# 3x3 convolution by tiles of 4x4 outputs for four images at once, in place of 4x2 outputs for two

**Chip, cores, metric.** One core of a Trainium2 chip. The time is that of one execution on the device in microseconds (us); the kernel before was run three times for its time and once with the profiler, every other kernel four times, one of them with the profiler, beside the kernel before on the same chip. The rounds ran on several chips, on which the median of the kernel before lay between 2524.8 and 2529.0 us: runs of different rounds are compared by their ratio to it, and a few us between their medians are not read as a difference.

## The reference, cut

Two bottleneck blocks, fp32, on 16 images of 1024 channels and 32x32 pixels. The first has local attention over 3x3 neighbours in its middle (32 heads of 8 channels), the second a 3x3 convolution of 256 channels.

```python
# layer 0
h = relu(bn(conv1x1(x, w_conv1)))                      # 1024 -> 256
q, k, v = relu(bn(conv1x1(h, wq))), relu(bn(conv1x1(h, wk))), bn(conv1x1(h, wv))
attn = softmax(einsum('bgdhw,bgdkhw->bgkhw', q, unfold3x3(k) + pos), axis=2)
a = relu(bn(einsum('bgdkhw,bgkhw->bgdhw', unfold3x3(v), attn)))
r = relu(bn(conv1x1(a, w_conv3)) + x)                  # 256 -> 1024
# layer 1
h1 = relu(bn(conv1x1(r, w1)))                          # 1024 -> 256
y = relu(bn(conv3x3(h1, w2)))                          # 256 -> 256, padding 1
out = relu(bn(conv1x1(y, w3)) + r)                     # 256 -> 1024
```

## The kernel before: the parts concerned

The program is one list of stages in TensorE's order. P is one image's projections (first 1x1, then q and k, then v; written C, Q, V when split), F a fused stage (256 to 1024, residual, and 1024 to 256 of layer 1), W a 3x3 stage, U the outputs of one image. While TensorE runs them, VectorE does the attention of other images "beside" them; a small model in the generator (`Side`) reckons with constants where VectorE will be, and so decides where each of its jobs goes in the programs' orders. Every engine and every transfer queue works in its own order: in the trace of the changed kernel TensorE's 6152 passes, VectorE's 1633 operations and ScalarE's 871 activations start in the order of their programs, by source line, and so do the 275, 490 and 512 transfers that ScalarE, SyncE and GpSimd issue.

The 3x3 convolution is done on transformed data (Winograd's method): weights (U) and input (V, the "form") are transformed, TensorE multiplies them, and VectorE transforms the products back to y. Other names in the profile lines: x is the input, h the output of a first 1x1, kp, bnk and bnv are keys and values on their way through DRAM (the "relay", which rearranges them), a is the attention's result, s a tile that holds the residual and then a fused stage's output, r the stored residual or the output, z a copy of products out of PSUM, diag a diagonal matrix for scaling the output weights. A "seed" is ScalarE's copy of the residual into PSUM, to which TensorE then adds. A "joint" is a place where one stage passes into the next.

```python
NI, NU = 6, 4                       # 6x4 products for a tile of 4x2 outputs
TR, TC = H // 4, W // 2
hpool: bufs=3 (8 KB)   ppool: bufs=4 (8 KB)   zpool: bufs=1, sized by tag

"P0 P1 P2 P3 F0 P4 C5 F1 Q5 W0 V5 U0 U1 F2 P6 C7 F3 Q7 W2 V7 U2 U3",
"F4 P8 F5 C9 Q9 W4 V9 U4 U5",
# ... [cut]
"F14 F15 U13:45 W14 U13:67 U14 U15",

# the form of the input is made piece by piece beside the products of its own stage
def along(t):
    v = ppool.tile([P, NU, NW * 2, TILES], F32, tag="t", name="v")
    # ... [cut: four VectorE operations with steps of two over the pixels]

# products: one product's 2 x 2 blocks of channels; 2 images x 128 tiles = 256 columns a pass
nc.tensor.matmul(acc[i][:, at, n, :], pieces[key][:, m, column % 2, n * P : (n + 1) * P],
                 vs[i][:, j, 2 * m : 2 * m + 2, :].rearrange("p b t -> p (b t)"), ...)

# end of a 3x3 stage, in the program's order
following[0][0].seed(following[0][1])      # ScalarE: residual into PSUM for the next output
finish_winograd(b)                         # ScalarE: batch norm and relu over y, two passes
if then:
    following[1][0].seed(following[1][1])
    finish_winograd(b + 1)

# logits of the attention end with
nc.vector.tensor_tensor(e, e, mx..., ALU.subtract)
yield None
nc.scalar.activation(e, e, AF.Exp)         # ScalarE, in its own order
```

Of the kernel before, what the change touches and what calls it, by code (L numbers as in the profile page):

```python
# [35 lines left out]
NI, NU = 6, 4  # L36
TR, TC = H // 4, W // 2
TILES = TR * TC
# [24 lines left out]
def sa_bottleneck_kernel(ctx: ExitStack, tc: tile.TileContext, x, w1t, wqkvt, w3t, u1t, u2t, u3t, params, out):  # L63
# [7 lines left out]
    hpool = ctx.enter_context(tc.tile_pool(name="hpool", bufs=3))  # L71
    apool = ctx.enter_context(tc.tile_pool(name="apool", bufs=1))
    ppool = ctx.enter_context(tc.tile_pool(name="ppool", bufs=4))
    zpool = ctx.enter_context(tc.tile_pool(name="zpool", bufs=1))
# [8 lines left out]
    uw = dram.tile([NI, 2, P, NW, 2, WID], F32, tag="uw", name="uw")  # L83
    ws = dram.tile([2, 2, P, NW, C // 2], F32, tag="ws", name="ws")

    COLUMNS = (1, 2, 3, 0)
# [15 lines left out]
    def more_weights():  # L102
# [4 lines left out]
        t = wpool.tile([P, HW], F32, tag="w", name=f"{name}{half}_{of}")  # L107
# [7 lines left out]
        if of == 0 and name == "w1":  # L115
            for c in range(k):
                nc.sync.dma_start(view[:, c], src[:, c])
        else:
            nc.sync.dma_start(view, src)
# [79 lines left out]

    VROWS = H + 4  # L200
    vh = const.tile([P, NW * 2 * VROWS + 2, PW], F32, tag="vh", name="vh")

    scaled = {}

    def load_scaled():

        rooms = vh.rearrange("p r w -> p (r w)")
        for which, src in enumerate((w3t, u3t)):
            for half in range(2):
                at = rooms[:, (2 * which + half) * HW :][:, :HW].rearrange("p (n o) -> p n o", n=NW)  # L210
# [6 lines left out]
    def scale_weights(which):  # L217
# [3 lines left out]
        diag = ppool.tile([P, 2 * HW], F32, tag="t", name="diag")[:, :C]  # L221
# [17 lines left out]

    taps = []  # L240

    def load_taps():
        n = 3 * WID
        for m in range(NW):
            pool, tag = ((ppool, "t"), (hpool, "h"))[m]
            first, second = (pool.tile([P, 2 * HW], F32, tag=tag, name="g") for _ in range(2))
            g = first[:, :n], first[:, n : 2 * n], second[:, :n]
            for i in range(3):
                nc.scalar.dma_start(g[i], u2t[m * P : (m + 1) * P, i * n : (i + 1) * n])
            taps.append(g)  # L250

    made = []

    def store_winograd_weights(of):
        for _ in range(of):
            m, i, half, u = made.pop(0)
            nc.sync.dma_start(uw[i, half][:, m], u)

    def winograd_weights():
        n = 3 * WID  # L260

        rooms = []
        for pool, tag, shape, of in (
            (apool, "e", [P, KK, JPIX], 1), (apool, "pc", [P, NPOS, JPIX], 1),
            (apool, "bnv", [P, HEAD_DIM, HALO], 1), (zpool, "tv", [P, NW * 2 * (TR + 1), PW], 2),
            (zpool, "m1", [P, NW, 2 * TILES], 4), (zpool, "s", [P, NW, 2 * TILES], 2), (wpool, "w", [P, HW], 2),
        ):
            for _ in range(of):
                t = pool.tile(shape, F32, tag=tag, name="u", **({"bufs": of} if pool is zpool else {}))
                if len(shape) == 3:  # L270
                    t = t.rearrange("p a b -> p (a b)")
                elif len(shape) == 4:
                    t = t.rearrange("p a b c -> p (a b c)")
                size = t.shape[1]
                rooms += [t[:, at : at + 2 * WID] for at in range(0, size - 2 * WID + 1, 2 * WID)]
        third, fourth = (ppool.tile([P, 2 * HW], F32, tag="t", name="g") for _ in range(2))
        s, t = third[:, :n], third[:, n : 2 * n]
        two = fourth[:, :n], fourth[:, n : 2 * n]
        small = third[:, 2 * n : 2 * n + WID], third[:, 2 * n + WID : 2 * n + 2 * WID]

        def both(dst, s, t, by):

            for to, op in zip(dst, (ALU.add, ALU.subtract)):
                nc.vector.scalar_tensor_tensor(to, s, by, t, ALU.mult, op)
# [844 lines left out]
```

## Time and profile before

| kernel before | |
|---|---|
| time | 2526.98 us, median of 3 runs (2520.68 to 2528.53) |
| span of the profiled run | 2520.6 us |
| TensorE / VectorE / ScalarE busy | 2470.8 / 1955.5 / 924.5 us |
| TensorE idle | 49.8 us |
| granted TensorE clock, mean | 0.998 |
| DMA | 638.9 MB, 253 GB/s |

The lines themselves, and how they are read, are in the prediction.

### The profile page before, as it was taken

To read this page: it belongs to the slowest core of one execution; us is meant where nothing else is said; L and a number is where in the kernel's file an instruction comes from. 1 tells how busy PE (TensorE), PEld (TensorE's weight loads), DVE (VectorE), ACT (ScalarE), POOL (GpSimd) and SP (SyncE) were. 2 spreads that over 40 slices of the span, in tenths; PEclk is the share of its full clock that TensorE was granted. 3 is DMA by queue.
4 is the path that set the end of the run, shared out by engine and by line. 5 is a ranking of instruction groups with operands and counts; after the bars stand their busy time and mean duration, and the time that the engine had idled before them with its cause. 6 is when DMAs were issued, how large, how long until landed. Compare 5 with 4: busy or idle time off the path is not lost.

```text
span 2520.6 us, 18901 instructions
## 1 busy us (share of the span) xinstructions
PE 2470.8 (98%) x6536; PEld 1224.1 (49%) x6536; DVE 1955.5 (78%) x1791; ACT 924.5 (37%) x891; POOL 239.5 (10%) x451
## 2 busy tenths in 40 slices
PE   7999999999999999999999999999999999899999
PEld 3443444644455444554445544455445544464464
DVE  6897999899989898989979991899814980993070
ACT  1224133552335524254232542325432533345335
POOL 1020110011000110001110011100100010001000
PEclk9999999999999999999999999999999999999999
DMA  8977677696776977678686777767767768658546
GB/s 304 352 252 258 232 266 238 208 371 235 265 246 228 344 243 259 219 256 327 230 276 228 274 258 252 253 220 273 278 211 236 255 233 269 218 200 303 189 150 234
DMA packets 244719, 638.87 MB, mean 253 GB/s; under 512 B 18576, under 2 KB 125328, under 8 KB 236432
## 3 DMA queue, kind: packets, MB, share of 16 engines
q0 software_dynamic: 63360, 266.89, 30.7%
q1 hardware_dynamic: 141152, 227.83, 28.4%
q10 hardware_dynamic: 40112, 142.94, 14.0%
q8 instruction: 53, 0.87, 0.1%
q14 instruction: 42, 0.34, 0.0%
HBM read 408.47 MB, written 229.11 MB: 253 GB/s over the span
## 4 chain that ended last, share of the span: by engine, by line
PE 84%; DVE 10%; DMA 3%; ACT 2%; issue 1%; ACTq 0%; SPq 0%; DVEq 0%; POOLq 0%
PE ps L387 31%; PE ps L356 30%; PE ps L738 12%; PE ps L437 10%; DVE prod L545 2%; DMA bnk<-kp 2%; DVE acc L609 1%; DVE term L597 1%; PE ps L480 1%; DVE v L665 1%; DVE prod L549 1%; DMA bnk<-bnk 1%; ACT h L956 1%; DVE tv L659 1%; DVE prod L550 1%
## 5 line engine op out<-in xcount | busy, mean ns | idle before, releaser
L356 PE MATMUL ps<-s,u 128*128 128x512 f32 x1024 | 458.4, 592 | 4.3 <-ACT s L400 4.3
L387 PE MATMUL ps<-a,w 128*128 128x512 f32 x1024 | 457.7, 592 | 0.0
L356 PE MATMUL ps<-x,w 128*128 128x512 f32 x1024 | 444.5, 595 | 9.5 <-DMA x<-in_x_dram 9.5
L387 PE MATMUL ps<-y,u 128*128 128x512 f32 x1024 | 441.6, 592 | 3.1 <-ACT ps L380 3.1
L545 DVE TENSOR_TENSOR prod<-qc,bnk 128x2048 f32<-128x2048 f32 x144 | 328.9, 2284 | 137.3 <-DMA bnk<-bnk 136.7
L738 PE MATMUL ps<-v,U 128*128 128x256 f32 x1536 | 338.1, 382 | 18.3 <-issue 7.3
L738 PEld LDWEIGHTS ps<-v,U 128*128 128x128 f32 x1536 | 292.4, 191 | 66.6 <-issue 13.1
L356 PEld LDWEIGHTS ps<-x,w 128*128 128x128 f32 x1024 | 195.4, 191 | 255.3 <-issue 244.9
L356 PEld LDWEIGHTS ps<-s,u 128*128 128x128 f32 x1024 | 194.3, 190 | 250.3 <-issue 235.1
L387 PEld LDWEIGHTS ps<-y,u 128*128 128x128 f32 x1024 | 194.4, 190 | 247.8 <-issue 222.4
L387 PEld LDWEIGHTS ps<-a,w 128*128 128x128 f32 x1024 | 194.6, 190 | 244.9 <-issue 226.0
L400 ACT ACTIVATE s<-ps,par 128x1024 f32<-128x1024 f32 x128 | 142.4, 1112 | 449.8 <-PE ps L387 449.8
L609 DVE TENSOR_TENSOR acc<-acc,term 128x2048 f32<-128x2048 f32 x128 | 293.3, 2292 | 4.4
L597 DVE TENSOR_TENSOR term<-e,bnv 128x2048 f32<-128x2048 f32 x128 | 292.2, 2283 | 0.0
L437 PE MATMUL ps<-h,wqk 128*128 128x512 f32 x512 | 230.4, 598 | 6.1 <-ACT h L956 6.1
L549 DVE TENSOR_TENSOR prod<-prod 128x1024 f32<-128x1024 f32 x144 | 176.3, 1224 | 4.9
L659 DVE SCALAR_TENSOR_TENSOR tv<-vh 128x1224 f32<-128x1224 f32 x32 | 45.0, 1426 | 167.8 <-ACT vh L990 167.8
L400 ACT ACTIVATE r<-ps,bn_sh 128x1024 f32<-128x1024 f32 x128 | 141.9, 1109 | 80.1 <-PE ps L387 79.4
L956 ACT ACTIVATE h<-ps,par 128x1024 f32<-128x1024 f32 x32 | 38.5, 1204 | 338.6 <-PE ps L356 338.6
L437 PEld LDWEIGHTS ps<-h,wqk 128*128 128x128 f32 x512 | 94.7, 190 | 138.9 <-issue 114.4
L380 ACT ACTIVATE ps<-s 128x1024 f32<-128x1024 f32 x128 | 131.4, 1027 | 56.4 <-ACT s L400 39.8
L335 POOL DMA_DIRECT2D r<-r x128 | 67.5, 528 | 888.5 <-DMA out_dram<-r 364.4
(93 smaller groups left out, 1725.5 us busy)
## 6 DMA issues: line engine op xcount, KB each, us to landing
s<-in_x_dram POOLq DMA_DIRECT2D x128, 512.0 KB, 5.8
r<-s ACTq DMA_DIRECT2D x128, 512.0 KB, 3.8
r<-r POOLq DMA_DIRECT2D x128, 512.0 KB, 5.0
out_dram<-r ACTq DMA_DIRECT2D x128, 512.0 KB, 6.1
x<-in_x_dram POOLq DMA_DIRECT2D x120, 512.0 KB, 4.3
U<-uw SPq DMA_DIRECT2D x96, 512.0 KB, 3.8
bnk<-kp SPq DMA_DIRECT2D x32, 680.0 KB, 7.2
bnv<-kp SPq DMA_DIRECT2D x32, 680.0 KB, 6.8
```

Of the source, the lines that this page charges most:

```text
L335: (nc.scalar if kind == "x" and b == 0 else nc.gpsimd).dma_start(t, src)
L356: nc.tensor.matmul(ps[n][:, halves(half)], wt[:, c % (NC // 2), n * P : (n + 1) * P], src[:, halves(half)], start=(c == 0), stop=(c == NC ...
L380: nc.scalar.activation(ps, t, AF.Identity)
L387: nc.tensor.matmul(self.ahead[o][:, halves(half)], pieces[key][:, n, o % (NC // 2) * P :][:, :P], self.src[:, n, halves(half)], start=Fals ...
L400: nc.scalar.activation(t, self.ahead.pop(o), RELU, bias=self.shift(o), scale=1.0)
L437: nc.tensor.matmul(ps[:, halves(half)], pieces[key][:, m, at : at + P], h[:, m, halves(half)], start=(m == 0), stop=(m == NW - 1),)
L545: nc.vector.tensor_tensor(by_row(t), by_row(qc), kc[:, :, i : i + JROWS, j : j + W], ALU.mult)
L549: nc.vector.tensor_add(t[:, 0:4], t[:, 0:4], t[:, 4:8])
L597: nc.vector.tensor_tensor(by_row(dst), rows(e[:, k, :]).unsqueeze(1).to_broadcast([P, HEAD_DIM, JROWS, W]), vc[:, :, i : i + JROWS, j : j ...
L609: nc.vector.tensor_add(acc, acc, t)
L659: nc.vector.scalar_tensor_tensor(to, a, by, b, ALU.mult, ALU.add)
L738: nc.tensor.matmul(acc[i][:, at, n, :], pieces[key][:, m, column % 2, n * P : (n + 1) * P], vs[i][:, j, 2 * m : 2 * m + 2, :].rearrange("p ...
```

## The change

The intent is a shorter TensorE stream: tiles of 4x4 outputs need a quarter fewer products, and with four images at once a pass keeps its 256 columns (the count is in the prediction). To make the form of the input contiguous for VectorE, layer 1's pixels are kept by their column's place in a tile (columns 0, 4, 8... first); ScalarE makes this order on the way out of PSUM. The form is now made right behind each fused stage, stored to DRAM and loaded when the 3x3 stage comes; images 13 and 14 are put off through a stash in DRAM. The buffers are cut anew, the forming of the 3x3 weights is interleaved with the first projections, and the exponential is issued by the model of VectorE.

```diff
-NI, NU = 6, 4
-TR, TC = H // 4, W // 2
-TILES = TR * TC
+NI = 6
+NK = 4
+TR = H // 4
+TILES = TR * TR
-    hpool = ctx.enter_context(tc.tile_pool(name="hpool", bufs=3))
+    hpool = ctx.enter_context(tc.tile_pool(name="hpool", bufs=5))
-    ppool = ctx.enter_context(tc.tile_pool(name="ppool", bufs=4))
-    zpool = ctx.enter_context(tc.tile_pool(name="zpool", bufs=1))
+    ppool = ctx.enter_context(tc.tile_pool(name="ppool", bufs=2))
+    zpool = ctx.enter_context(tc.tile_pool(name="zpool", bufs=3))
... [cut: weights' forming with ScalarE steps, weight pieces shared between stages]
         def result(self, o, to):
             t = self.tiles.pop(o)
-            nc.scalar.activation(t, self.ahead.pop(o), RELU, bias=self.shift(o), scale=1.0)
+            ps, to_ = self.ahead.pop(o), t
+            if self.kind == "s":
+                ps, to_ = ps.rearrange("p (n j) -> p j n", j=4), t.rearrange("p (j n) -> p j n", j=4)
+            else:
+                ps, to_ = ps.rearrange("p (j n) -> p n j", j=4), t.rearrange("p (n j) -> p n j", j=4)
+            nc.scalar.activation(to_, ps, RELU, bias=self.shift(o), scale=1.0)
... [cut: attention's adds by two taps]
-        yield None
-        nc.scalar.activation(e, e, AF.Exp)
-        yield 3.0
+        yield lambda: nc.scalar.activation(e, e, AF.Exp)
... [cut: the form, 24 operations of 612 or 816 elements, and its store]
+                nc.sync.dma_start(
+                    room[:, at // 2, :, b % NK, at % 2].rearrange("i p e -> p i e"),
+                    u.rearrange("p (i e) -> p i e", i=NI),
+                )
... [cut: products of four images, the way back on VectorE]
+    DEFERRED = 13, 14
... [cut]
+        "P0 P1 P2 P3 F0 P4 F1 P5 P6 F2 P7 F3 C8 Q8 W0 V8 U0 U1 U2 U3",
+        "F4 P9 F5 P10 F6 F7 C11 Q11 W4 V11 U4 U5 U6 U7",
+        "F8 P12 F9 P13 F10 F11 C14 Q14 W8 V14 U8 U9 U10:0123",
+        "F12 P15 F13 F14 F15 U10:4567 U11:012345 W12 U11:67 U12 U13 U14 U15",
... [cut]
+            if made:
+                finish_winograd(made.pop(0))
             cost = next(parts)
... [cut]
             following[0][0].seed(following[0][1])
             finish_winograd(b)
+            made.extend(range(b + 1, b + NK))
             if then:
                 following[1][0].seed(following[1][1])
-                finish_winograd(b + 1)
+                finish_winograd(made.pop(0))
```

## The prediction

> **What bounds the kernel now.** I read the page's busy shares and slices first, then its chain, the groups by line, the chain in order of time around one 3x3 stage, and last the stretches of 3x3 and output stages.
>
> ```profile
> PE 2470.8 (98%) x6536; PEld 1224.1 (49%) x6536; DVE 1955.5 (78%) x1791; ACT 924.5 (37%) x891; POOL 239.5 (10%) x451
> PE 84%; DVE 10%; DMA 3%; ACT 2%; issue 1%; ACTq 0%; SPq 0%; DVEq 0%; POOLq 0%
> ```
>
> TensorE is busy 2470.8 of 2520.6 us and is 84% of the chain: only what shortens its stream, or the 49.8 us in which it idles, is worth time. VectorE's 78% is a mean over stages, and matters where TensorE waits for it.
>
> ```profile
> L738 PE MATMUL ps<-v,U 128*128 128x256 f32 x1536 | 338.1, 382 | 18.3 <-issue 7.3
> L665 DVE TENSOR_TENSOR v<-tv 128x512 f32<-128x512 f32 x192 | 120.1, 687 | 2.3
> L659 DVE SCALAR_TENSOR_TENSOR tv<-vh 128x1224 f32<-128x1224 f32 x32 | 45.0, 1426 | 167.8 <-ACT vh L990 167.8
> L400 ACT ACTIVATE r<-ps,bn_sh 128x1024 f32<-128x1024 f32 x128 | 141.9, 1109 | 80.1 <-PE ps L387 79.4
> ```
>
> L738 is the 3x3 convolution of layer 1; the 382 ns of one is latency of a pipelined instruction, its pace must come from the chain:
>
> ```profile
> 432.02 41.44 PE ps L738 x192
> 473.46 6.87 PE ps L437 x16
> ...
> 2194.74 1.12 ACT r L400
> 2195.86 0.82 issue
> 2196.69 3.75 PE ps L738 x8
> ```
>
> 192 passes in 41.44 us are 0.2158 us a pass of 256 columns; 16 passes of 512 in 6.87 us are 0.429. The last lines are one of the few places where TensorE waited: a 3x3 stage that began late. Each 3x3 stage is followed by outputs:
>
> ```profile
> 432.00:473.50 41.50, 41.50 (x194) 36.53 (x193) 37.27 (x61) 10.52 (x17) 0.00 (x0) 1.00 0.58 170
> 480.30:542.10 61.80, 61.80 (x146) 27.36 (x145) 56.08 (x33) 42.54 (x40) 9.99 (x19) 1.00 0.99 362
> ```
>
> The columns are PE, PEld, DVE, ACT, POOL busy, clock, DMA share, GB/s. Both stretches keep TensorE full. The 3x3 stage has DMA to spare (0.58); the output stage has none (0.99).
>
> [...]2048 elements 2284 to 2292[...], 512 elements 687 to 692[...], for adds with two inputs and scaled sums alike. [...]Steps of two fp32 cost nothing here (L665 steps by two, 687 ns, the contiguous L550 692); a step of four, which the change brings to ScalarE's PSUM reads, no row shows. [...]the highest 20 us stretch here has 421 GB/s at a share of 1.02.
>
> **The change, part by part.** Tiles of 4x4 outputs in place of 4x2 need 36 products per 16 outputs where 24 per 8 stood. Four images (4x64 tiles) keep 256 columns a pass. Built, the program has 576 matmuls there in place of 768, two passes each.
>
> TensorE. Before 1536 x 0.2158 = 331.5 us (8 stages of 41.44), after 1152 x 0.2158 = 248.6 (4 of 62.2): **82.9 us less**. All other matmuls are the same in number and size. Their stages from the chain: one image's projections 50.83 us (71.62 to 122.45), fused stage 128 x 0.4293 = 54.95, outputs 64 x 0.4293 = 27.47. 16 x 133.25 + 331.5 = 2463.5, so 57.1 of the span lies outside the streams: about 20 at both ends and in the start (9.5 first input, 2.6 slow clock, 3.3 for the scale row, some 5 after the last matmul), the rest around the 3x3 stages and in small waits. After: 2132.0 + 248.6 = **2380.6, plus 20**.
>
> VectorE. Attention's adds go by two taps: 144 x (1224+692+425) = 337 us becomes 64 x 4208 + 16 x 2341 = 307: -30. The form was 256 us (rows of v and tv); it becomes 12 ops of 612 and 12 of 816 per image, 21.6 us, 346 in all: +90. The way back was 157 us (rows of y, m, s); per group of four it becomes 6 x 1.224 + 18 x 0.692 + 12 x 0.685 + 32 x 0.692 + 2 x 2.29 = 54.7 us, 219 in all: +62. Sum 1955.5 + 122 = some 2077, 84% of the new span. It remains second. Adding stages up, attention finishes well before its fused stage except for image 15: two fused stages and the value projection (117 us) stand between its queries and its use, against 13 for the relay, 94.2 of attention and some 15 back: about 5 us of wait.
>
> The 3x3 stage itself. A part is 16 passes, 3.45 us. VectorE's 54.7 us fit into 62.2 only if evenly spread, and they are not: it can start at 11.5 us (second copy out), and the middle pair brings 22 us (two sums of 2048, sixteen updates, the tile sums) after its last product at 41.4, so it ends at 58. The third pair's second tile sum then frees the copy buffer (three, each shared) late: the last part waits until 61.6, not 58.7: **2.9 us**. The y are complete from 71 us on, TensorE ends at 65.1, the value projection covers up to 72. Then ScalarE has, in program order, two finishing passes (1.23 each) for each of four images, two kp and two seeds between them, so the third output waits for its seed until about 85 where it could have begun at 79: **6.5 us**. In all 9.4 per stage, some 12 for the last one, which has two output parts as cover: **41 us in four**. Before, such ends were hidden because two images finish in half the ScalarE time.
>
> The entry of a 3x3 stage. Form and DRAM round trip replace the form beside the products. After the fourth image: 2.4 (vh) + 21.6 + about 8 (three v buffers, so two pairs wait for their store to land) + 5 store + 5 load = 42 us; the projections between are 43.6. It fits. For the last group only 10 output parts (34.3 us) lie between: **8 us**.
>
> DMA. The form stores 40.1 MB and loads 40.1; U loads fall by 12.6 MB, output weights by 4.2, stashes of two images add 5.3, the rest +1.3: 638.9 becomes some 709 MB, 288 GB/s. In the 3x3 stage U and V need 36 tiles of 0.53 MB, 14 of them fetched ahead: with the next stage's prefetch about 256 GB/s, against 170 before. Outputs of four images then run 110 us on end at the share of 0.99 that they had for 62.
>
> Sum: 2380.6 + 20 + 41 + 8 + 5 + 8 (kp, halo and other small waits; the old ones around 220 and 2190 us were of that size) = 2462.6 for the span; runs lie some us above it or at it. **I predict 2462 us**, 2.6% less: the gain of 83 is partly given back, about 20 us, at the joints.
>
> **Rivals.** (1) *The whole gain arrives.* If the author's order hides the ends (VectorE's rows overlap by some per cent: the rows add up to 1999, busy is 1955), the four stages lose 3 us each, not 10: 2425 to 2435. For it: before, TensorE waited only 18.3 us at L738 although VectorE had 37.3 of 41.5 us there. Against it: in the schedule's own bookkeeping the part is set at 0.8 us more than a chunk of 3.43, 14 us a stage, as if it had been seen to take longer. (2) *DMA becomes the bound in outputs.* 0.99 for 62 us was sustained with TensorE full; over 170 us with 74,000 new packets of 544 B and V loads ahead of the residuals in one queue, each delay lands on TensorE. Ten per cent of 4 x 110 us would give 2505. (3) *ScalarE's stepped reads.* All 256 output activations now read PSUM by steps of 4 or 256 elements. At twice 1.11 us, an output part has 3.2 of 3.43 us on ScalarE: the backlog after the 3x3 lasts longer, +15 us; at three times, outputs are bound by it: above 2530. (4) *VectorE becomes the bound*: against it stand its 84% and the slack found by adding stages; it would show as waits of fused stages, 2490.
>
> **Range and chances.** The sure part is 83 us of TensorE. Joints can cost from 15 us (rival 1, 2430) to 75 (rival 2 or 4). Range **2428 to 2508**. A 2% gain ends at 2476: faster 0.63, same 0.32, slower 0.05 (needs rival 3 at its worst).
>
> **What would show it.** L738's successor with 1152 passes at 0.216 us within a part; TensorE busy near 2386 (2470.8 less 84.5, a quarter of 338.1); VectorE near 2077; rows of form 795 and of v 1007 ns; DMA near 709 MB. In each 3x3 stage a wait before its last part, and one of some 6 us at the third output after it, ended by ScalarE behind y. A wait of about 8 us before the last 3x3. I am wrong if passes run slower than 0.216 (four runs of 64 columns), if output activations take over 1.5 us, if TensorE waits for residual loads, or if fused stages wait for attention.

The times by number of elements are VectorE's, in ns. The 795 and 1007 for rows of 612 and 816 elements are estimates: the straight line through the measured 690 for 512 elements and 2288 for 2048 gives 794 and 1006.

## The result

The changed kernel takes **2512.66 us** (median of 4, 2511.27 to 2515.97) where the kernel before took 2527.30 in the same rounds. The ratio is 0.9949, 95% interval 0.9929 to 0.9969; ratios here are the mean time of one kernel's runs over that of the other's of the same rounds, so not quite the ratio of the medians. So 0.5% faster, not the 2.6% predicted, and outside the range; by the 2% limit of the prediction's own chances this is "same", to which it gave 0.32.

First the page after, busy times and chain:

```profile
PE 2413.9 (96%) x6152; PEld 1158.9 (46%) x6152; DVE 2081.9 (83%) x1633; ACT 928.3 (37%) x873; POOL 275.2 (11%) x523
PE 72%; DVE 15%; DMA 7%; ACT 4%; issue 1%; SPq 0%; ACTq 0%; DVEq 0%; POOLq 0%
```

TensorE's share of the chain fell from 84 to 72%: VectorE, DMA and ScalarE took it. The costs of single instructions came out as predicted. The chain in order of time shows a run of the 3x3 stage (start, us, what). The groups by shape show the output activations and the form (count | busy us, mean ns of one | idle time before, and what ended it):

```profile
712.48 41.45 PE ps L732 x192
```

```profile
L403 ACT ACTIVATE s<-ps,par 128x1024 f32<-128x1024 f32 x128 | 142.3, 1112 | 433.5 <-PE ps L384 426.3 <-DMA r<-s 5.8 <-DMA v<-v 1.4
...
L663 DVE SCALAR_TENSOR_TENSOR v<-v 128x816 f32<-128x816 f32 x48 | 48.4, 1008 | 1.7
...
L663 DVE SCALAR_TENSOR_TENSOR form<-form 128x612 f32<-128x612 f32 x48 | 38.2, 796 | 1.6
```

192 passes, each now to four separate runs of 64 columns, still take 41.45 us (41.44 before), ScalarE reads PSUM by steps of 4 elements in 1112 ns (the same group took 1112 in order before; the other group, by steps of 256, takes 1107, before 1109), the form's rows take 1008 and 796 ns (1007 and 795 estimated). VectorE has 2082 us (2077 predicted), DMA moves 708.9 MB (709). The 82.9 us of TensorE did go. Its busy time fell by only 56.9, though, and its idle time doubled:

| TensorE, us | before | after |
|---|---|---|
| its streams at full pace (2463.5, 2380.6: the prediction's sums) | 2463.5 | 2380.6 |
| busy time lost to a clock below 1 | 3.1 | 22.6 |
| rest of the busy time | 4.2 | 10.7 |
| idle | 49.8 | 96.2 |
| span | 2520.6 | 2510.1 |

The second row is an estimate, busy time x (1 - granted clock), summed over stretches of 10 us (stretches of 2 us give 24.7 after). The first row counts some idle time twice: the 50.83 us that the prediction takes for one image's projections hold 0.44 us in which TensorE waits for h, so about 7 us of the idle row are in the streams too, and the rest of the busy time is about 7 us larger, before and after alike. The differences stand. So of 82.9 us won, 72.4 are given back: 46.4 as idle time, 19.5 as slow clock, 6.5 in the rest. What TensorE waited for, in us, times and longest:

```profile
PE ps L353 <- ACT s L403: 20.2, 5, 13.0
PE ps L384 <- ACT ps L377: 18.4, 11, 3.3
PE ps L732 <- ACT z L755: 13.3, 5, 3.0
PE row L236 <- DVE diag L229: 12.1, 2, 6.7
PE ps L353 <- DMA x<-in_x_dram: 8.6, 1, 8.6
...
PE ps L732 <- DMA U<-uw: 5.6, 3, 3.7
PE ps L384 <- ACT a L638: 3.7, 2, 2.5
```

None of the first four was so large before (s 4.3, seeds 3.1, copies 3.9, diagonals 3.3). Stretch by stretch, with the columns PE, PEld, DVE, ACT and POOL busy, clock, DMA share (the mean busy share of the core's 16 DMA engines) and GB/s:

```profile
60.00:80.00 20.00, 8.57 (x14) 3.68 (x15) 12.05 (x24) 7.93 (x18) 1.05 (x2) 0.74 1.03 353
80.00:100.00 20.00, 20.00 (x44) 8.69 (x43) 17.04 (x20) 1.45 (x4) 2.62 (x5) 0.92 1.00 380
2140.00:2160.00 20.00, 14.27 (x34) 6.03 (x32) 19.55 (x16) 2.14 (x2) 1.05 (x2) 0.96 0.27 94
2160.00:2180.00 20.00, 12.76 (x24) 5.58 (x25) 17.54 (x12) 10.66 (x9) 0.53 (x1) 0.70 0.65 245
```

Both are places where TensorE stands for some us and then runs at a clock between 0.7 and 0.96. The later one, in the order of time (start, us, engine, line, operation; in brackets the idle time before it and what ended it):

```profile
2099.07 0.53 POOL L529 DMA_DIRECT2D bnk<-bnk  x1 [15.77 <-issue]
...
2112.66 4.49 DVE L548 TENSOR_TENSOR prod<-qc,bnk 128x2048 f32<-128x2048 f32 x2 [35.03 <-DMA bnk<-bnk]
...
2159.16 2.56 DVE L577 TENSOR_TENSOR e<-e,mx 128x2304 f32<-128x2304 f32 x1
2161.75 2.12 ACT L580 ACTIVATE e<-e 128x2304 f32<-128x2304 f32 x1 [18.63 <-DVE e L577]
```

```profile
2167.24 6.07 PE L353 MATMUL ps<-s,u 128*128 128x512 f32 x8 [12.96 <-ACT s L403]
```

The last store of image 15's keys was issued at 2086.05, and their way through DRAM and back took 26.6 us (the model has 13): 13.0 until the load was issued, 13.6 until it had landed. VectorE idled 35.0 us for them. ScalarE's program had the exponential of this image ahead of the last sums of fused stage 13 and the first output of fused stage 14, as if VectorE were 18.6 us further on; ScalarE stood before it, and TensorE behind ScalarE. The end of the last 3x3 stage:

```profile
2375.02 1.02 ACT L755 ACTIVATE z<-ps 128x1024 f32<-128x1024 f32 x1 [7.70 <-DVE z L758]
2376.09 5.41 PE L732 MATMUL ps<-V__2_8223,U 128*128 128x256 f32 x16 [2.98 <-ACT z L755]
2384.92 2.37 ACT L818 ACTIVATE y<-y,bn_sh,bn_inv 128x1024 f32<-128x1024 f32 x2 [7.96 <-DVE y L797]
2387.20 1.00 ACT L377 ACTIVATE ps<-r 128x1024 f32<-128x1024 f32 x1
2388.25 4.63 PE L384 MATMUL ps<-y,u 128*128 128x512 f32 x5 [3.32 <-ACT ps L377]
```

The last part waits 2.98 us for a copy of the tile sums, and its 16 passes then take 5.41 us where 3.45 is the pace (a record of 16 passes at full pace reads 3.6 to 3.7); the granted clock is 0.64 from 2376.2 to 2381.0. In the first 3x3 stage of the same run the same wait of 2.98 us was followed by passes at full pace, with a clock of 1.00:

```profile
774.16 3.72 PE L732 MATMUL ps<-V__2_2598,U 128*128 128x256 f32 x16 [2.98 <-ACT z L755]
```

Of the four stages, the second and the last show the slow passes (5.41 us both, clock 0.67 and 0.64), the first and the third do not (3.72 us both, clock 1.00). In the last stage ScalarE then idles 7.96 us before y, with a seed whose data are long there standing behind y in its order; TensorE waits for that seed.

### The profile page after: what moved, and what is told of

It reads as the page before. It is cut to its first block, busy times and chain, and to the rows that moved or that the text cites. A ratio compares the mean times of both kernels' runs of the same rounds, so it can differ in the third digit from the quotient of the medians.

```text
span 2510.1 us, 18335 instructions
## 1 busy us (share of the span) xinstructions
PE 2413.9 (96%) x6152; PEld 1158.9 (46%) x6152; DVE 2081.9 (83%) x1633; ACT 928.3 (37%) x873; POOL 275.2 (11%) x523
## 4 chain that ended last, share of the span: by engine, by line
PE 72%; DVE 15%; DMA 7%; ACT 4%; issue 1%; SPq 0%; ACTq 0%; DVEq 0%; POOLq 0%
PE ps L353 30%; PE ps L384 26%; PE ps L439 10%; PE ps L732 6%; DVE acc L599 2%; DVE acc L612 2%; DVE y L758 2%; DVE prod L548 2%; DMA bnk<-kp 1%; DMA U<-uw 1%; ACT y L818 1%; DMA u<-in_u1t_dram 1%; PE ps L481 1%; DMA a<-a 1%; DVE z L758 1%
## 5 line engine op out<-in xcount | busy, mean ns | idle before, releaser
L353 PE MATMUL ps<-s,u 128*128 128x512 f32 x1024 | 464.5, 599 | 20.3 <-ACT s L403 20.2
L384 PE MATMUL ps<-y,u 128*128 128x512 f32 x1024 | 451.3, 602 | 18.5 <-ACT ps L377 18.4
L548 DVE TENSOR_TENSOR prod<-qc,bnk 128x2048 f32<-128x2048 f32 x144 | 324.1, 2288 | 36.9 <-DMA bnk<-bnk 35.0
L599 DVE TENSOR_TENSOR acc<-e,bnv 128x2048 f32<-128x2048 f32 x144 | 327.7, 2285 | 3.8
L384 PEld LDWEIGHTS ps<-a,w 128*128 128x128 f32 x1024 | 194.9, 191 | 250.6 <-issue 226.7
L403 ACT ACTIVATE s<-ps,par 128x1024 f32<-128x1024 f32 x128 | 142.3, 1112 | 433.5 <-PE ps L384 426.3
L612 DVE TENSOR_TENSOR acc<-acc 128x2048 f32<-128x2048 f32 x128 | 293.4, 2292 | 4.4
L403 ACT ACTIVATE r<-ps,bn_sh 128x1024 f32<-128x1024 f32 x128 | 141.8, 1107 | 77.6 <-PE ps L384 76.7
L553 DVE TENSOR_TENSOR prod<-prod 128x2048 f32<-128x2048 f32 (+1 forms) x80 | 166.2, 2078 | 2.5
L377 ACT ACTIVATE ps<-r 128x1024 f32<-128x1024 f32 x128 | 131.3, 1026 | 72.5 <-ACT r L403 39.8
L329 POOL DMA_DIRECT2D x<-in_x_dram x120 | 63.5, 529 | 688.6 <-PE ps L353 491.2
L329 POOL DMA_DIRECT2D s<-in_x_dram x128 | 67.6, 528 | 544.6 <-PE ps L353 335.5
L451 ACT ACTIVATE kp<-ps,par 128x1024 f32<-128x1024 f32 x64 | 77.3, 1207 | 128.0 <-PE ps L439 79.5
```

The costliest lines, as they stand in the source:

```text
L329: (nc.scalar if kind == "x" and b == 0 else nc.gpsimd).dma_start(t, src)
L353: nc.tensor.matmul(ps[n][:, halves(half)], wt[:, c % (NC // 2), n * P : (n + 1) * P], src[:, halves(half)], start=(c == 0), stop=(c == NC ...
L377: nc.scalar.activation(ps, t, AF.Identity)
L384: nc.tensor.matmul(self.ahead[o][:, halves(half)], pieces[key][:, n, o % (NC // 2) * P :][:, :P], self.src[:, n, halves(half)], start=Fals ...
L403: nc.scalar.activation(to_, ps, RELU, bias=self.shift(o), scale=1.0)
L451: nc.scalar.activation(dst, src, func, bias=col(f"L0_conv_{name}_b", n), scale=col(f"L0_conv_{name}_s", n),)
```

## The experiments

Nineteen kernels, of which one did not fit into memory and never ran (four copy buffers without making room). "Theory A" and "B" are named anew in each expectation. The main theory after reading the traces: **the gain is given back at joints, where work that waits for VectorE stands in front of ready work in the order of ScalarE or of a queue, and idle time is often followed by a slow clock.** Rivals: the transfers (709 MB, small packets) are the bound; VectorE's amount of work is; or single waits as such cost, wherever they stand.

| run | median us | ratio to before | 95% interval |
|---|---|---|---|
| changed kernel | 2512.66 | 0.9949 | 0.9929 to 0.9969 |
| e1_exp_later | 2514.52 | 0.9958 | 0.9941 to 0.9975 |
| e2_scale_early | 2517.50 | 0.9978 | 0.9943 to 1.0012 |
| e4_more_cover | 2515.12 | 0.9958 | 0.9929 to 0.9988 |
| e5_p15_early | 2502.93 | 0.9911 | 0.9895 to 0.9926 |
| e6_y_behind | 2500.94 | 0.9906 | 0.9891 to 0.9920 |
| e8_forming_on_vector | 2518.33 | 0.9975 | 0.9960 to 0.9990 |
| e9_none_deferred | 2491.79 | 0.9865 | 0.9845 to 0.9884 |
| c1_both (e6 and e9) | **2480.67** | **0.9816** | 0.9802 to 0.9831 |
| c2_four_copies (on c1) | 2482.69 | 0.9826 | 0.9810 to 0.9843 |
| c3_start (on c1) | 2486.28 | 0.9842 | 0.9827 to 0.9857 |
| c4_v_stores (on c1) | 2494.66 | 0.9868 | 0.9852 to 0.9885 |
| d1_less_vector (on c3, wrong result) | 2453.75 | 0.9705 | 0.9691 to 0.9720 |
| d2_u_queue (on c1) | 2498.22 | 0.9879 | 0.9864 to 0.9894 |
| d3_u_queue_start (on c3) | 2491.73 | 0.9856 | 0.9841 to 0.9871 |
| d4_relay20 (on c1) | 2483.00 | 0.9820 | 0.9805 to 0.9834 |
| d5_kept_warm (on c1) | 2485.37 | 0.9843 | 0.9820 to 0.9866 |
| d6_gpsimd_scale (on c3) | 2514.75 | 0.9942 | 0.9926 to 0.9959 |
| f1_less_vector_only (wrong result) | 2496.96 | 0.9890 | 0.9873 to 0.9906 |

### Image 15: the exponential, or the attention that is late

```diff
 # e1_exp_later: for image 15 alone the exponential is issued 20 us later by the model
+        def due(self):
+            return self.exp[0] + (20.0 if self.jobs[0]["b"] == B - 1 else 0.0)
-                if self.exp and self.exp[0] < self.tensor + 4.0:
+                if self.exp and self.due() < self.tensor + 4.0:
... [cut: two more places that ask due() in place of exp[0]]
```

> Edit: for image 15 alone the exponential is put some nine ScalarE instructions later in ScalarE's program order (behind the fourth output of fused stage 14), so that ScalarE no longer stands 18.6 us in front of work that TensorE needs. Theory A (the place of the exponential in ScalarE's order is what costs time there): the 13.0 us wait of TensorE for s is gone, and the slow clock behind it (8 us), so 15 to 20 us less, about 2494. Theory B (the attention of image 15 starts late, at 2112.7 us, because its relay through DRAM took 26.6 us where the schedule's model has 13; its end at 2222 sets fused stage 15 anyway): the wait only moves to the start of fused stage 15, 0 to 4 us less, about 2510. I hold B.

No gain. The wait changed its name; what TensorE waited for in the profile of this run, all between 2130 and 2230 us:

```profile
PE ps L384 <- ACT a L638: 18.8, 1, 18.8
```

The 13.0 us stall is gone, and fused stage 15 now waits 18.8 us for its attention (3.7 before). The exponential's place was the wait that the profile named, not the cause: the attention's end set the time, as theory B had it. The 18.8 us also fit the prediction's own sum with one term put right: it had 5 us of wait with a relay of 13 us, and the relay took 13.6 us longer.

```diff
 # e5_p15_early
-        "F12 P15 F13 F14 F15 ...
+        "P15 F12 F13 F14 F15 ...
-        if b == B - 1:
+        if b == B - 1 and DEFERRED[0] in kept:
 # e9_none_deferred: the same order, and
-    DEFERRED = 13, 14
+    DEFERRED = ()
```

> Edit: the projections of image 15 stand ahead of fused stage 12, not behind it. Theory B (image 15's attention is late, and with it the exponential in ScalarE's order and fused stage 15): VectorE no longer idles 35 us before it; the 13.0 us wait for s, the 3.7 us for a and the slow clock behind them go: 16 to 26 us less, about 2490. Theory C (the DMA queues are full there, share 1.0 from 2066 to 2120, whatever stands in them; the relay and the stores of the form only collide elsewhere): less than 6 us gained, with new waits for weights or residuals in fused stage 12.

> Edit: projections of image 15 ahead of fused stage 12 as in the earlier run (2502.9 us), and no image's form is put off any more: each is made right behind its fused stage. Theory A (in that run the last 3x3 stage started some 9 us late, because VectorE had three forms, 65 us, left after image 15's attention): that wait falls to 0 to 3, the time by 7 to 12 against that run, about 2493. Theory B (VectorE is the bound in the last three fused stages, attention and forms together): fused stages 14 and 15 wait instead for vh or for attention, within 4 us of 2503.

With the projections early, waits for a are gone from the list and those for s fall from 20.2 to 7.7 us:

```profile
PE ps L353 <- ACT s L403: 7.7, 4, 4.7
```

Still, only 10 us are won (2502.93): the last 3x3 stage now begins with 8.9 us of idle time in the stretches around 2290, because three forms are still to be made. With no form put off this falls to 2.9, and the time to 2491.79: 21 us won in all. The cause of the loss at image 15 is shown: its queries were projected one fused stage too late for the attention's real way, and the putting off of two forms, which was to make room for it, cost as much at the next joint.

### The ends of the 3x3 stages: y, cover, copies

```diff
 # e4_more_cover
-U10:4567 U11:012345 W12 U11:67 U12
+U10:4567 U11:0123 W12 U11:4567 U12
 # e6_y_behind
-            if made:
-                finish_winograd(made.pop(0))
             cost = next(parts)
+            if made and (made[0] % NK == 0 or part == 4):
+                finish_winograd(made.pop(0))
...
             following[0][0].seed(following[0][1])
-            finish_winograd(b)
-            made.extend(range(b + 1, b + NK))
+            made.extend(range(b, b + NK))
             if then:
                 following[1][0].seed(following[1][1])
-                finish_winograd(made.pop(0))
```

> Edit: two more output parts of image 11 are kept back to stand between the last 3x3 stage and the first output of its own images (four instead of two). Theory A (the end of a 3x3 stage costs time because y is not finished when TensorE could begin): the loss of 6.6 us after the stage (2360 to 2400) and the 1.5 us of slow clock fall to 0 to 3: 4 to 8 us less in all. Theory B (ScalarE has seeds, outputs and eight finishing passes to do in that stretch and is what is too slow; more cover only brings it more work): 0 to 2 us less.

> Edit: at the end of a 3x3 stage ScalarE's program order is changed and nothing else: the finishing pass of the first image's y stands behind the part that follows, not ahead of the seeds, keys and outputs of it; those of the other three images stand in the middle of the output stage before their own. Theory A (TensorE waits there because ready seeds stand in ScalarE's order behind a y that VectorE has not finished; in the last stage ScalarE idled 8.0 us so): the wait for seeds falls from 18.4 us to under 8, the idle time after the four 3x3 stages from 28 to some 12 to 16: 12 to 18 us less with the slow clock, about 2497. Theory B (y itself is late, VectorE ends it): the wait moves to y, 0 to 5 us less.

More output parts as cover gave nothing: TensorE still waited three times, 6.1 us, for seeds in that place. The seeds of the cover itself stood behind y. Putting y behind the part gave 12 us (2500.94). The idle time after the four 3x3 stages fell from 28.5 to 12.0 us, which are the four waits of 3.0 us for copies; what TensorE waited for of seeds in the whole run fell from 18.4 us to

```profile
PE ps L384 <- ACT ps L377: 12.5, 7, 6.4
```

So what cost time was the order in ScalarE, as theory A had it (though the seeds' waits did not fall below the 8 us that it named). This run also shows a wait that was not there before; the order of time, first ScalarE's queue for transfers, then ScalarE and TensorE:

```profile
1403.21 0.34 ACTq L404 DMA_DIRECT2D out_dram<-r  x1
1403.60 1.03 ACT L377 ACTIVATE ps<-r 128x1024 f32<-128x1024 f32 x1 [9.73 <-DMA a<-acc]
...
1404.68 7.67 PE L384 MATMUL ps<-y,u 128*128 128x512 f32 x13 [6.40 <-ACT ps L377]
```

ScalarE had its output r ready at 1393.9 but issued its store only at 1403.2, when the store of an attention result by SyncE, issued at 1391.82, had landed. The built program of this run shows why: its 765 transfers issued by SyncE and by ScalarE take eight semaphores strictly in turn, and before each issue its engine waits for the landing of the one that had its semaphore before. The store that waited (output 5 of image 5) takes the semaphore that the attention's store had, eight issues earlier. The trace of the changed kernel has the same: the landings of its 765 such transfers are told by eight semaphores, 96 or 95 each, and every transfer was issued after the landing of the one that had its semaphore before, the closest 0.02 us after it. A slow transfer of one queue so stops the other engine, here for 9.3 us. In the changed kernel ScalarE waits some 27 us in all for landings of other tiles' transfers (attention 17.7, forms 4.7, weights 4.3); before, 18.7 of the 19.5 us that it waited for transfers in front of seeds were for the seeds' own data. Three successive issues of ScalarE in the built program as an example, each with the semaphores that it waits for (the wait for the DMAHW one is an instruction of its own in front of the issue):

```
L404 DMACopy out_dram<-r_4_3_4672 128x1024 [waits DMAHW7_49,Activation_49]
L404 DMACopy out_dram<-r_4_4_4686 128x1024 [waits DMAHW0_49,Activation_49]
L404 DMACopy out_dram<-r_4_5_4704 128x1024 [waits DMAHW1_49,Activation_49]
```

```diff
 # c2_four_copies: c1_both, and
-zpool bufs=3   CHUNKS = 8
+zpool bufs=4   CHUNKS = 7
```

> Edit: the run before this one (both edits) with four instead of three shared 4 KB buffers and seven instead of eight pixel tiles (an earlier kernel with four buffers alone did not fit and never ran). Theory A (the four waits of 3.0 us before the last part of each 3x3 stage, and the slow clock that shows behind each, are a cost of their own): the waits for z go from 11.9 to below 3 us, 10 to 16 us less than the run before. Theory B (VectorE ends y at the same time; seven pixel tiles make residual loads late): 0 to 4 less, or more time.

No gain on c1_both (2482.69 against 2480.67): the four waits of 3.0 us for copies are gone, and TensorE waits for seeds (19.1, was 11.8), for y (3.8, was none) and for s (14.6, was 7.9) instead. That fits B, VectorE's end of y sets this joint; seven pixel tiles show too, in ScalarE's waits for residuals (23.0 us, was 3.2), so the two are not told apart cleanly.

### Both edits together

> Edit: the two edits that gained by themselves together: ScalarE's order at the end of the 3x3 stages (2500.9), and image 15's projections early with no form put off (2491.8); the changed kernel has about 2513. If the two losses are independent joints, their gains of some 12 and 21 us add up: 2476 to 2484. If instead each only lets TensorE run into the next limit (ScalarE's output issues that wait for the landing of other transfers, seen once at 1394 to 1403 us in the first of the two), 2486 to 2492.

2480.67 us: 32 us less than the changed kernel, close to the sum of 12 and 21. So the two gains add up. This version beats both kernels, 1.84% faster than before by the ratio (the interval is 1.69 to 1.98%), 1.3% faster than the changed one (0.9816 / 0.9949).

### The start

```diff
 # e2_scale_early
-        hooks["v", 0, 0] = lambda: (scale_weights(0), side.passes(3.4))
-        hooks["v", 0, 1] = lambda: (scale_weights(1), side.passes(3.4))
+        hooks["conv1", 0, NC - 1] = lambda: (scale_weights(0), side.passes(3.4))
+        hooks["qk", 0, 0] = lambda: (scale_weights(1), side.passes(3.4))
 # e8_forming_on_vector
-            nc.scalar.activation(t0, a[1], AF.Identity, scale=-1 / 6)
+            nc.vector.tensor_scalar(t0, a[1], -1 / 6, None, ALU.mult)
... the other three ScalarE steps likewise
 # c3_start: c1_both, and the diagonals and small matmuls split off from scale_weights
-        hooks["v", 0, 0] = lambda: (scale_weights(0), side.passes(3.4))
-        hooks["v", 0, 1] = lambda: (scale_weights(1), side.passes(3.4))
+        hooks["conv1", 0, 2] = lambda: (scale_rows(0), scale_rows(1), side.passes(1.7))
+        hooks["conv1", 0, 6] = lambda: (scale_weights(0), scale_weights(1), side.other(9.2))
```

> Edit: the scaling of the output weights (two diagonals, four matmuls, four products on VectorE) is put where the first 1x1 convolution ends, ahead of most of the 3x3 weights' forming, not in the middle of it. Theory A (the start loses its time because these matmuls stand in TensorE's order and wait for VectorE, which waits for buffers of the forming): the second image's projections start at 71 to 74 us, not 82.25; the time falls by 8 to 12 us, TensorE's busy time by 1 to 3 of these. Theory B (the forming is what everything waits for; DMA is at a share of 1.0 there): the wait comes back at the next thing, less than 3 us gained.

> Edit: the forming of the 3x3 weights at the start runs on VectorE alone, as before the change; its ScalarE steps are scalings and copies on VectorE. Theory A (the forming is slow because each of its steps passes through ScalarE's order, behind keys that wait for their store, 8.4 us): second image's projections start at 72 to 77 us, not 82.25; 6 to 10 us less. Theory B (the store of formed weights, 7.8 us to landing and few buffers, or VectorE's own order sets it): 0 to 3 us less.

> Edit: both edits, and at the start the diagonals and the four small matmuls of the weight scaling are put ahead of all forming (VectorE makes the diagonals at about 6 us; the matmuls stand behind the third input part), the products that use them behind the seventh. Nothing of TensorE then waits for the forming. Theory A (at the start the order of VectorE, diagonals behind the forming, holds TensorE up for 12 us): the second image's projections start at 70 to 73 us, the wait for diagonals goes, 8 to 14 us less than both edits alone. Theory B (image 0's and 1's attention, which starts when the forming ends, holds the first fused stage up by as much more): 0 to 4 us less, with the wait at about 230 us grown.

e2 moved the wait from 60-80 us to 40-60 us (9.9 us for diagonals) and pushed image 0's attention from 89.8 to 100.2; the second projections start at 82.39 as before (82.04 after the change). e8 made it worse, 85.16: VectorE then was busy 48 of 60 us, and the diagonals stood behind more work. c3 took the diagonals out of the way altogether: TensorE has no idle time over 0.9 us in any stretch of 10 us between 20 and 690, the second projections start at 65.06. All the same it is 5.6 us slower than c1_both (same rounds, no overlap of the runs), which neither theory foresaw. The lead over c1_both can be followed at the ends of the 3x3 stages: 764.0 against 779.4 us, 1324.9 against 1336.1, 1895.2 against 1901.1, 2361.4 against 2353.2. It shrinks at each, and the last one costs more than is left. Stretches of c3_start in front of its first 3x3 stage (columns as above):

```profile
640.00:660.00 20.00, 20.00 (x48) 8.81 (x47) 19.62 (x19) 2.58 (x2) 0.53 (x1) 1.00 0.16 52
660.00:680.00 20.00, 19.56 (x46) 8.49 (x45) 18.65 (x15) 4.81 (x4) 2.09 (x4) 1.00 0.73 228
680.00:700.00 20.00, 16.49 (x66) 11.08 (x64) 19.66 (x13) 6.41 (x6) 4.19 (x8) 1.00 1.04 413
700.00:720.00 20.00, 14.61 (x60) 12.66 (x61) 10.15 (x15) 1.02 (x1) 1.58 (x3) 0.83 1.01 372
```

VectorE is full, DMA idles at 0.16, then everything comes at once and TensorE stands. SyncE waited 26.0 us there for VectorE's v, whose store was next in its order. Two readings remain: order in the queues, or VectorE's pace.

### Queues, or VectorE's pace

```diff
 # c4_v_stores: c1_both, and the store of the form
-                nc.sync.dma_start(
+                nc.gpsimd.dma_start(
 # d2_u_queue: c1_both, d3_u_queue_start: c3_start, and
+        elif name[0] == "U":
+            nc.gpsimd.dma_start(view, src)
 # d1_less_vector: c3_start, f1_less_vector_only: the changed kernel; wrong result on purpose
-            nc.vector.tensor_add(acc, acc, t)
+            if k % 2:
+                nc.vector.tensor_add(acc, acc, t)
```

> Edit: both edits, and the 96 stores of the form go through GpSimd's queue, not SyncE's. Stores of the form wait in SyncE's order for VectorE, and the loads of U, the stores of keys and attention stand behind them; besides, ScalarE's output issues wait for the eighth transfer before them of either of the two queues. Theory A (this coupling costs time): waits for U (5.9 to 8.4 us) fall below 3, ScalarE's waits for landings of other tiles' transfers (some 27 us in the changed kernel) halve: 4 to 10 us less than both edits alone. Theory B (the total traffic sets it, or GpSimd's queue, with x and residual loads behind the stores, gets the same trouble): within 3 us, or slower with waits for x and s.

> Edit: both edits (2480.7), and the 72 loads of the 3x3 weights go through GpSimd's queue, where nothing waits for VectorE's form but the form's own loads. Theory A (these loads are late because they stand behind stores of the form in SyncE's order): the wait for U (4.8 us) goes; 2 to 6 us less. Theory B (GpSimd's queue holds the loads of the form, which wait longer): 0 less, or more time.

> Edit: both edits, the early start, and the 3x3 weights' loads through GpSimd's queue. Theory A (queue order): the 27.4 us of waits for U in the run with the early start fall below 10, 8 to 16 us less than its 2486.3, thus below the 2480.7 of both edits alone. Theory B (VectorE's pace): the waits stay, now for the form's own loads, within 5 us of 2486.

> A wrong result on purpose. Edit: the kernel with both edits and the early start (2486.3), where the 16 us won at the start were gone again by the end; every second sum of the weighted values is left out, 4 x 2.29 us of VectorE per image, 147 us in all. Theory A (with TensorE freed, VectorE and what hangs on its order is the pace between the 3x3 stages: it is 92 to 96 per cent busy there): the waits for U loads, which stand in the queue behind stores that wait for VectorE (27.4 us), and the 10.1 us for image 15's attention fall together below 12 us; 18 to 30 us less than 2486. Theory B (the transfers themselves, a burst at a share of 1.04 in front of each 3x3 stage, set these waits whatever VectorE does): 0 to 8 us less.

> A wrong result on purpose. Edit: the changed kernel itself, nothing mended, with every second sum of the weighted values left out (147 us of VectorE). Theory A (it is mostly the amount of VectorE's work that gives the gain back): the stall of 13 us behind the exponential, the waits at the ends of the 3x3 stages and the first fused stage all shrink: 25 us less or more, 2488 or below. Theory B (it is mostly where waiting work stands in ScalarE's and VectorE's orders, which this leaves as it is; the seeds behind y, the exponential, the diagonals): the start and the ends of the 3x3 stages keep their losses, only image 15's end comes earlier: 8 to 18 us less, 2495 to 2505. I hold B for this kernel and A for the mended one.

No other distribution of the transfers helped: 14 us slower (c4), 17.6 slower (d2), and d3 is 5.5 above c3, which is not clear of noise (the intervals overlap). In d3 the 27.4 us of waits for U became 12.4, with 15.6 "issue" at the same line: same joint, other name. With 147 us of VectorE's work gone, c3_start becomes **32.5 us** faster (2453.75), more than theory A's 18 to 30. First c3_start, then d1_less_vector, what TensorE waited for at the first product of a piece:

```profile
PE ps L736 <- DMA U<-uw: 27.4, 5, 8.9
```

```profile
PE ps L737 <- DMA U<-uw: 10.2, 5, 3.6
...
PE ps L390 <- ACT a L643: 2.5, 1, 2.5
```

(a was 10.1 in c3_start.) So in c3_start, where the start no longer does, VectorE sets the pace at 84% of the span: it is busy 192.5 of the 200 us from 100 to 300, 211.9 of 220 from 780 to 1000, 226.7 of 250 from 1000 to 1250, and the idle time that makes the mean look harmless lies inside the 3x3 stages, where it waits 61.7 us for copies. One reserve: leaving sums out also shortens each attention's latency; amount and latency are not told apart. For the changed kernel as it was, f1 gave only 15.7 us, and every joint kept its wait: seeds 21.3 (18.4), the stall behind the exponential 12.1 (13.0), diagonals 11.9 (12.1), copies 11.9 (13.3). There the order at the joints was the larger part, as I held (c1_both, with the order mended at two of them, won 32 us).

### Two smaller questions

```diff
 # d4_relay20: c1_both, and
-    CHUNK, RELAY, EXP, LATE = 3.43, 13.0, 3.0, 30.0
+    CHUNK, RELAY, EXP, LATE = 3.43, 20.0, 3.0, 30.0
 # d6_gpsimd_scale: c3_start, and
-        nc.vector.tensor_mul(acc, acc, se.unsqueeze(1).to_broadcast([P, HEAD_DIM, JPIX]))
+        nc.gpsimd.tensor_mul(acc, acc, se.unsqueeze(1).to_broadcast([P, HEAD_DIM, JPIX]))
```

> Edit: both edits (2480.7), and the one constant with which the schedule reckons the trip of keys and values through DRAM is 20 instead of 13 us (the trip of image 15 took 26.6 us in the changed kernel, the medians of its two transfers are 7.7 and 10.8). Theory A (work of VectorE is put into the programs' orders earlier than it can run, and other work stands behind it): the small waits for s and seeds fall, 3 to 8 us less. Theory B (the order matters only where it blocked, and those places are mended): within 3 us.

> Edit: the kernel with both edits and the early start (2486.3); the last product of each image's attention (2.29 us, 37 us in all) runs on GpSimd instead of VectorE, with a correct result. After the run with 147 us less of VectorE (32.5 us faster) theory A (VectorE's pace) has some 0.22 us won per us taken away: 5 to 10 us less, about 2478. Theory B (GpSimd waits in order for VectorE and holds back the loads behind it, as the stores of the form did there, or is so slow that the way to the fused stage grows): no gain, 2484 to 2496, with waits for x, s or a.

d4 is within 3 us: a truer constant gains nothing once the two places are mended. d6 is 28.5 us slower than c3_start. Theory B foresaw no gain, but not this loss, and one part of it neither theory had: VectorE's busy time rose from 2079.7 to 2113.4 us although it had 37 us of work less. One place in the order of time:

```profile
186.17 8.79 DVE L554 TENSOR_TENSOR prod<-qc,bnk 128x2048 f32<-128x2048 f32 x2
186.34 6.48 POOL L618 TENSOR_TENSOR acc<-acc,se 128x2048 f32<-128x2048 f32 x1 [3.22 <-DVE acc L616]
```

The two products of VectorE, else 4.49 us, take 8.79 while GpSimd's product of 6.48 us runs. In this place the two lost 4.3 us. The totals fit: with the 37 us that it no longer had, VectorE was busy 70.7 us more, 4.4 us for each of the sixteen products on GpSimd (an estimate from these sums). How much of the 28.5 us this is was not separated: GpSimd's product takes 4.5 to 6.5 us where VectorE's took 2.29, and TensorE's waits for a (14.4 us, was 10.1) and for copies (24.5, was 11.9) grew too.

### Is the slow clock a consequence of the idling?

```diff
 # d5_kept_warm: c1_both, and ahead of the four small matmuls of scale_weights
+        for _ in range((60, 42)[which]):
+            nc.tensor.matmul(row[:, :P], ones, eye, start=True, stop=True)
```

> Edit: both edits (2480.7), and in front of the four small matmuls of the weight scaling TensorE runs 60 and 42 matmuls of 128 columns on constants, whose result is overwritten, to fill the two waits (7.2 and 5.0 us) without moving them. Theory A (the slow clock, 0.71 and 0.84 around these two waits, comes from TensorE's idling): the matmuls behind each wait take 1.7 us, not 3.75, the 16 behind the second start at full pace, the second image's projections start 2 to 5 us earlier than 82.9; the time falls by 2 to 5. Theory B (the clock is low there for another reason, as the load of the start): 3.75 us as before.

In the changed kernel, then in d5_kept_warm, the small matmuls behind the two waits:

```profile
66.04 3.64 PE L236 MATMUL row<-diag,ones 128*128 128x512 f32 x4 [6.68 <-DVE diag L229]
...
78.50 3.75 PE L236 MATMUL row<-diag,ones 128*128 128x512 f32 x4 [5.39 <-DVE diag L229]
```

```profile
72.25 1.88 PE L238 MATMUL row<-diag,ones 128*128 128x512 f32 x4
...
86.78 1.88 PE L238 MATMUL row<-diag,ones 128*128 128x512 f32 x4
```

Half the time, at full clock (granted 1.00 from 60 to 90 us; in the changed kernel 0.50 from 77 to 83): A holds, here. I had sized the filler wrongly (each matmul ran as two passes, the 60 as 120 and the 42 as 84; it ran 13.6 and 9.5 us in waits of 7.2 and 5.0), so the second projections started later, at 88.50, and nothing was won (2485.37 against 2480.67, with overlapping intervals). The length of a wait alone does not tell whether the clock falls: 2.98 us of waiting were enough in the last 3x3 stage (16 passes in 5.41 us, clock 0.64), while the same wait in the first one left the clock at 1.00. What decides between the two is not shown.

## Why the prediction was wrong, step by step

The prediction put 82 us of span on top of the streams; there were 129.5 (2510.1 - 2380.6). By its own terms:

| term | predicted | measured: idle + slow clock |
|---|---|---|
| both ends and the start | 20 | 25.5 + 3.7 |
| ends of the four 3x3 stages | 41 | 28.5 + 9.1 |
| entries of 3x3 stages | 8 | 7.0 + 2.9 |
| attention of image 15 | 5 | 16.7 + 4.1 |
| keys, halo and other small waits | 8 | 10.3 + 2.6, and 8.2 of scattered idle time (most of it for h) and 10.9 of the rest of the busy time |
| sum | 82 | 129.5 |

- **TensorE's 82.9 us less, the instruction costs, VectorE's 2077, 709 MB:** right, to within 0.3%. Rival 3 (stepped reads) is out: 1112 ns.
- **Ends of the 3x3 stages (41):** right in mechanism; the idle time was 28.5, and the sum of 37.6 comes near only with 9.1 of slow clock that the prediction did not reckon there. The prediction named a seed behind y and 2.9 us before the last part; the trace of the last stage has 3.32 (at the second output part, not the third) and 2.98. e6 shows that ScalarE's order was the cause of more than half of the idle time.
- **Entries (8):** the size came out by luck. The wait of 8 us was to stand before the last 3x3 stage, for the form's trip; there TensorE waited 1.0 us, and the largest wait, 4.6, stood before the third. These two were for loads of U, the second stage's 1.4 for a copy.
- **Image 15 ("about 5 us of wait"): the step that failed most at a single joint** (20.8 us, and 21 won back by experiment). The step reckoned 13 us for the relay, the schedule's own constant. In the kernel before, the medians of its two transfers were already 7.2 and 9.5 us; here, with DMA at a share of 1.04 from 2080 to 2100, it was 26.6. And it took a late attention as a wait at its own fused stage only. It first stopped ScalarE, and TensorE, one fused stage earlier. e1's 18.8 us agree with the sum with the relay put right; e5 and e9 show 21 us for this joint together with the putting off of forms.
- **The start (part of the 20):** the old values were carried over (3.3 for the row, 2.6 slow clock). Measured 12.1 and 3.7. The part of the diff that interleaves the forming with the first projections was not worked out at all. But e2, e8 and c3 show that these 12 us were not there to be won: what follows was no further.
- **The slow clock, 22.6 us where 2.6 was reckoned:** only the start's term had any (by the measure used here, the start of the kernel before lost 1.2 to 1.4). All other joints were priced by their idle time alone. The ratio to the idle time is no constant: 0.23 here (22.6 / 96.2), 0.06 in the kernel before (3.1 / 49.8), 0.16 in c3_start (13.3 / 83.6), 0.31 in e9 (25.1 / 80.4). d5 shows the link for the two waits it filled; for the others it is read from the traces.
- **Small waits (8):** mis-sized by more than any other term, 32.0 for 8; some 10 of the measured sum stood in the kernel before already (6.1 of waits for h, 4.2 of the rest of the busy time) and were not in the 8 that was carried over. (The waits for h are inside the 50.83 us of the streams, so that as much busy time again is hidden there; see the table of the result.)
- **Rival 4 (VectorE becomes the bound)** was set aside with its mean of 84% and "the slack found by adding stages". For the kernel as it was that held in the main (f1: 15.7 us); for the version with both joints and the start mended it sets the pace (d1: 32.5 us). **Rival 2 (DMA)** is not shown as a bound of its own: moving transfers between queues won nothing, and the bursts at a share of 1.04 looked at in c3_start came behind VectorE; no run had less traffic.

With the two mended joints (2480.67) the kernel is still 19 us above the predicted 2462. What these are stays in part open: d1 shows VectorE's pace as the limit for c3_start, but no such run was made of c1_both; how much is VectorE's amount and how much its latency is not told apart; and the start's 16 us can be moved but were not won.

## What to carry to other kernels

A shorter stream on the busiest engine is worth what the second engine's orders can follow: before adding up its gain, look for each joint where ready work stands in an in-order engine or queue behind work of the second engine, and for that engine's idle time, whether it lies where it could be used. When a wait is moved away and the time stays, the wait was a name and not the cause: ask what TensorE waits for next. Price a TensorE wait of some us with a slow clock that may stand behind it: over these kernels it came to between 0.06 and 0.31 us for each us of idle time.
